# The first thirty microseconds of an attention layer: identity matmuls before the tokens come, transposes by halves of the inputs, and another order of the first loads and weight sums

## The chip, the core and the metric

The kernel runs on one core of a Trainium2 chip. The core has five engines that run side by side, each with its own queue of instructions: TensorE (PE in the profile) multiplies matrices, VectorE (DVE) and ScalarE (ACT) work element by element, GpSimd (POOL) here mostly issues DMAs, and SyncE (SP) issues DMAs only. The metric is the device time of one execution in microseconds. The kernel before took a median of 1350.63 us in three runs (1345.75, 1350.63, 1352.09).

## The reference

A layer norm, an attention with rotary positions and a fixed rescaling of some keys, a small mixture of low-rank experts whose output is a gate, and a residual sum. Cut to what matters:

```
x = L0_attn_hidden_states                      # 8 sequences x 256 tokens x 512, float32
xn = (x - mean(x)) / sqrt(var(x) + 1e-5)
q, k, v = xn @ wq.T, xn @ wk.T, xn @ wv.T      # 32 query heads, 8 key/value heads, width 128
q, k = rope(q), rope(k)
scores = q @ k.T / sqrt(128) * key_scale + causal
s = (softmax(scores) @ v) @ wo.T
logits = xn @ router_w.T                       # 4 experts, the best 2 are kept
gates = softmax(top2(logits))
delta = sum_e gates_e * (xn @ A_e.T) @ B_e.T * 4
x = x + s * silu(delta)
```

## The kernel before

**Tiling.** The 8 sequences are taken in four pairs (`tb` 0 to 3). A pair's 512 tokens are four tiles of 128 tokens (`t` 0 to 3; tiles 0 and 1 are sequence `b` = 0, tiles 2 and 3 are `b` = 1). The normalised tokens are turned, so that the 512 inputs stand on partitions, into `XB[tb]`, four blocks of 128x512: sequence `b` by half `h` of the inputs. Everything is float32, and a float32 matmul shows as two records of PE in the trace, a transpose as one.

**Products.** Weights come in quads of four blocks (A11, A12, A21, A22; numbers 0, 1, 3 and 2 in the names). A quad is multiplied with the pair of sequences in the Strassen-Winograd manner, with seven products instead of eight (`quad`, pieces p1, p2, p6, p5, p7, p4, p3). That needs four sums of weight blocks (`blocks_of`: S1 = A21+A22 is block 4, S2 = S1-A11 block 5, S3 = A11-A21 goes into block 3, S4 = A12-S2 block 6) and four sums of token blocks (`add_up`: `XT` 0 to 3, the first is `XB` of sequence 1, half 0, less that of sequence 0, half 0). Both are made on VectorE. The weight sums are also written to memory by GpSimd for the later pairs ("sums<-w"). The first quad of all is that of the first four key heads, number 8: its product into bank pa is `pak` in the trace, into pd `pdk`, into pe `pek`. The first query quad follows (`paq`, `peq`, `pdq`; weights `w_0`), then the first value quad (`pav`, weights `w_10`).

**Order.** No engine's order is written by hand. The kernel hands jobs to a planner (`Plan`): each with an engine, a planned time (`takes`), the jobs that it comes after, the buffers that it opens and closes, and a lag until its result is there. TensorE's jobs get due times from the order in which they are laid (`lay`); the others' due times follow backwards from those. `Plan.run` then plays the program through with these numbers and emits, on each engine, the ready job that is due first. So a changed number or dependency can change the order of any queue. On the chip the engines run these fixed orders and wait for each other through semaphores.

**The start, for the first pair.** `norm(0)` loads the four tiles of x on SP's queue (`load`, line 325). VectorE takes each tile's statistics (st, mv), then for two tiles at a time a variance, ScalarE's square root and a reciprocal (rstd), and it normalises (`normalise`, xn, line 348). TensorE turns a tile with the identity in four transposes (`turn`, line 355, xp), and ScalarE copies the result out of PSUM (`read`, line 366). GpSimd writes the identity at about 1 us and later clears `probs_sb` (`clear`, line 1354; "MEMSET p" in the trace). SP issues, in this order: four x, then w_8 blocks 0, 1, 3, 2, then ra (router and expert weights), then w_0 blocks 0, 1, 3, 2. ScalarE's queue issues the loads of tab and bt (rope tables and expert weights) right after its first two copies.

VectorE's order at the start: statistics of tiles 0 and 1, xn 0, xn 1, statistics of tiles 2 and 3, the weight sum of block 4, the variance of tiles 2 and 3, the sum of block 5, the reciprocal, the sums of blocks 3 and 6, xn 2, xn 3, the first key output (`ck<-pek,p1k`), XT 0 to 3.

TensorE's order: transposes of tiles 0 and 1 (8), `pak` (block 0 with sequence 0, half 0), `pek` (block 1 with sequence 0, half 1), transposes of tiles 2 and 3 (8), the router's products for two tiles (`lme`, 16 records), `pdk` (block 4 with XT 0), `pak` (block 5 with XT 1), and so on.

All instructions but a few are recorded under line 118, a helper that keeps them in program order; they are told apart by their tiles.

Of the kernel before, what the change touches and what calls it, by code (L numbers as in the profile page):

```python
# [37 lines left out]
F32 = mybir.dt.float32  # L38
# [6 lines left out]
P = 128  # L45
B, S, D = 8, 256, 512
# [10 lines left out]
NT = TB // P  # L57
DC = D // P
# [111 lines left out]
class Plan:  # L170
# [10 lines left out]
    def add(self, engine, takes, what, after=(), opens=(), closes=(), near=None, lag=0.0):  # L181
        after = [a for a in after if a]
        job = Job(engine, takes, what, after, opens, closes, near, lag, len(self.jobs))
        for a in after:
            a.then.append(job)
        for hold in closes:
            hold.readers += 1
        self.jobs.append(job)
        return job

    def lay(self, job):
        job.due = self.laid
        self.laid += job.takes
# [63 lines left out]
def layer(ctx: ExitStack, tc: tile.TileContext, x, wquad, woquad, raT, bT, table, out):  # L257
    nc = InOrder(tc)
    pool = lambda name, bufs, **kw: ctx.enter_context(tc.tile_pool(name=name, bufs=bufs, **kw))
# [9 lines left out]
    ps_mm = pool("ps_mm", 4, space=PSUM)  # L269
    ps_sc = pool("ps_sc", 2, space=PSUM)  # L270
    ps_av = pool("ps_av", 2, space=PSUM)
    bounce = pool("bounce", 4, space=DRAM)
    turned = pool("turned", 2, space=DRAM)
# [3 lines left out]
    ra = keep.tile([P, DC, E + E * R], F32, tag="ra", name="ra")  # L277
    bt = keep.tile([E * R, O], F32, tag="bt", name="bt")
    ident = keep.tile([P, P], F32, tag="ident", name="ident")
# [11 lines left out]
    plan = Plan()  # L291
    add = plan.add
    rooms = {}

    def hold(tag):
        return Hold(rooms[tag])

    for tag, n in dict(
        mm=4, sc=2, av=2, x=XPAIRS, m=2, acc=ACC, side=3, w=RING, wo=RING_O, a=RING_A, c=2, sw=2, qT=3,
# [6 lines left out]
    gates, sums_of, acts, weights, x_hold, loaded = {}, {}, {}, {}, {}, {}  # L306
# [7 lines left out]
    def norm(tb):  # L314
# [4 lines left out]
        xs, box = {}, {}  # L319
        xh = [hold("x") for _ in range(NB)]  # L320
        mh = [hold("m") for _ in range(NT)]
        ph = [hold("mm") for _ in range(0 if tb else NT)]
        x_hold[tb] = hold("X")

        def load(t):
            if t % 2 == 0:
                xs["x", t // 2] = x_pool.tile([P, 2, D], F32, tag="x", name=f"x{tb}_{t}")
            xs[t] = xs["x", t // 2][:, t % 2, :]
            nc.sync.dma_start(out=xs[t], in_=x[bass.ds(tb * TB + t * P, P), :])
# [22 lines left out]
                op0=ALU.subtract, op1=ALU.mult,  # L352
            )

        def turn(t):
            pt = box["p", t] = ps_mm.tile([P, 2, 2, P], F32, tag="mm", name=f"xp{tb}_{t}")
            for c in range(DC):
                nc.tensor.transpose(pt[:, c // 2, c % 2, :], box[t][:, bass.ts(c, P)], ident)

        def new_acts():  # L360
            acts[tb] = (
# [1 line left out]
                one.tile([P, 4, 2, S], F32, tag="XT", name=f"XT{tb}"),  # L363
            )

        def read(t):
            if t == 0:
                new_acts()
            nc.scalar.copy(acts[tb][0][:, t // 2, :, :, bass.ts(t % 2, P)], box["p", t])

        def turn_blocks(t):

# [35 lines left out]
        issues = []  # L408
        for t in range(NT):
            issues.append(  # L410
                add("sp", 0.3, lambda t=t: load(t), after=issues[-1:],
                    opens=[xh[t // 2]] if t % 2 == 0 else [])
            )
        loads = [
            add("dma", 0.0, lambda: None, after=[issues[t]], lag=8.5 if tb else 3.9 + 0.5 * t)
            for t in range(NT)
        ]
        if not tb:
# [2 lines left out]
        xn = []  # L421
        for ts in [slice(0, NT)] if tb else [slice(0, 2), slice(2, NT)]:
# [8 lines left out]
            for t in tiles:  # L431
                xn.append(
                    add("dve", 0.45, lambda t=t: normalise(t), after=[inv], opens=[mh[t]],
                        closes=[xh[t // 2]])
                )
        reads, pieces = [], []
        if tb:
            for b in range(NB):
                turns = [
                    add("dve", 0.6, lambda t=t: turn_blocks(t), after=xn[2 * b : 2 * b + 2], closes=[mh[t], xh[b]])  # L440
                    for t in (2 * b, 2 * b + 1)
# [3 lines left out]
                    add("sp", 2.4, lambda b=b: gather(b), after=[out_] + reads[:1],  # L445
                        opens=[] if b else [x_hold[tb]], lag=7.0)
                ] * 2
        for t in [] if tb else range(NT):
            tp = add("pe", 0.5, lambda t=t: turn(t), after=[xn[t], identity], opens=[ph[t]], closes=[mh[t]])
            opens = [x_hold[tb]] if t == 0 else []  # L450
            after = [tp] + reads[:1]
            reads.append(
                add("act", 0.5, lambda t=t: read(t), after=after, opens=opens, closes=[ph[t]],
                    near=(tp, 0.5))
            )
            pieces.append(tp)
        t1 = add("dve", 0.61, lambda: add_up(0), after=reads)
# [4 lines left out]
        if not tb:  # L462

            loaded["ra"] = add(
                "sp", 0.3, lambda: nc.sync.dma_start(out=ra, in_=raT), after=issues, lag=6.0
            )
            loaded["turned"] = pieces[-1]
            loaded["tab"] = add("act", 1.0, load_tables, after=reads[:1], lag=6.0)
        return pieces

# [2 lines left out]
    def blocks_of(tb, room, ring, source, kept, key, form, first):  # L473


        n = f"{room}{tb}_{key}"
        box, there, holds = {}, {}, {}
        order = (A11, A12, A21, A22, S1, S2, S4) if first else form.order
        if not tb and not first:
            order = (A11, A21, A22, A12, S1, S2, S4)  # L480

        def load(i):
            w = box[i] = ring.tile([P, 2, 2 * P], F32, tag=room, name=f"{n}_{i}")
            k = form.sums.index(i) if tb and i in form.sums else None
            src = source[:, i] if k is None else kept[:, k].rearrange("p (c m) -> p c m", c=2)
            (nc.sync if first else nc.gpsimd).dma_start(out=w, in_=src)

        def sum_up(i):
            to, a, b, op = form.steps[i]
            if to not in box:  # L490
                box[to] = ring.tile([P, 2, 2 * P], F32, tag=room, name=f"{n}_{to}")
            getattr(nc.vector, op)(box[to], box[a], box[b])

        def keep_sum(i):
            k = form.sums.index(i)
            nc.gpsimd.dma_start(
                out=kept[:, k].rearrange("p (c m) -> p c m", c=2), in_=box[i]
            )

        for i in order:  # L500
            holds[i] = hold(room)
        if tb:
            for i in order:
                after = [sums_of[room, key, i]] if i in form.sums else []
                there[i] = add("pool", 0.8, lambda i=i: load(i), after=after, opens=[holds[i]], lag=6.0)
            return box, holds, there
        issue = list(first)
        for i in order[:4]:
            there[i] = add(
                "sp" if first else "pool", 0.4 if first else 0.8, lambda i=i: load(i), after=issue,  # L510
                opens=[holds[i]], lag=6.0,
            )
        for i, (to, a, b, op) in enumerate(form.steps):
            there[to] = add(
                "dve", 0.61, lambda i=i: sum_up(i), after=[there[a], there[b]] + form.before(i, there),
                opens=[holds[to]] if to in order[4:] else [], closes=[holds[a], holds[b]],
            )
        for i in form.sums:
            sums_of[room, key, i] = add(
                "pool", 0.8, lambda i=i: keep_sum(i), after=[there[i]], closes=[holds[i]],  # L520
                lag=5.0,
            )
        return box, holds, there

    class Features:


        order = (A11, A12, S2, S1, S3, A22, S4)
# [10 lines left out]
    class Outputs:  # L539


        order = (A11, A21, S2, S1, A12, S4, A22)
# [10 lines left out]
    def quad(tb, which, out, room, rows, name):  # L553

        wbox, wh, there = blocks_of(
            tb, "w", w_pool, wquad[which], sums[which], which, Features,
            [] if len(weights) > 1 else begun,
        )  # L560
        weights[tb, which] = True
        box = {}
        new = lambda what: ps_mm.tile([P, 2, S], F32, tag="mm", name=f"{what}{name}")
        XB, XT = acts[tb, "B"], acts[tb, "T"]
        pa, pd, pe = hold("mm"), hold("mm"), hold("mm")
# [19 lines left out]
        def piece(bank, i, half, b, t, first, after):  # L585
            return add(
                "pe", 1.73, lambda: product(bank, i, half, b, t, first),
                after=[there[i]] + (XB[2 * b : 2 * b + 2] if t is None else [XT[t]]) + after,
                opens=[{"pa": pa, "pd": pd, "pe": pe}[bank]] if first else [],
                closes=[wh[i], x_hold[tb]],  # L590
            )
# [14 lines left out]
        if not tb:  # L606
# [6 lines left out]
            closes=[pe, s1], near=(p2, 1.0),  # L613
# [8 lines left out]
            closes=[s3], near=(p7, 1.0),  # L622
# [4 lines left out]
            closes=[pa], near=(p4, 0.0),  # L627
# [4 lines left out]
            near=(p3, 1.0),  # L632
# [565 lines left out]
    def experts(tb):  # L1198
# [3 lines left out]
        box = {}  # L1202
# [62 lines left out]
        routes = []  # L1265
        for t in range(NT):
            routes.append(
                add("pe", 0.94, lambda t=t: route(t),
                    after=[acts[tb, "B"][t], loaded["ra"], loaded["turned"]] + routes[:1],
                    opens=[] if t else [lh], closes=[x_hold[tb]])  # L1270
            )
        p1 = routes[-1]
# [3 lines left out]
            after=[r1], near=(p1, 4.0),  # L1276
# [77 lines left out]
    def clear():  # L1354
        nc.gpsimd.memset(probs_sb, 0.0)

    identity = add("pool", 1.5, lambda: make_identity(tc.nc, ident), near=None)
    cleared = add("pool", 2.0, clear)

    LAG_V = 2  # L1360
# [4 lines left out]


    tiles = norm(0)
    lead = []
    for q in quads[0]:
# [5 lines left out]
    for n in range(len(steps) + 2):  # L1375
        last = n >= len(steps)
        tb, g = (NTB, 0) if last else steps[n]
# [67 lines left out]
```

## Time and profile before

| | |
|---|---|
| median of three runs | 1350.63 us (1345.75 to 1352.09) |
| profiled execution | 1350.19 us, its span 1348.4 us, mean granted clock 0.998 |
| TensorE busy | 1325.3 us, 98% of the span |
| weight loads busy | 1165.7 us, 86% |
| VectorE, ScalarE, GpSimd busy | 82%, 45%, 23% |
| first transpose, first matmul, first record of pdk | 6.64, 9.35, 19.19 us from the span's start |
| landing of the last w_8 block | 11.19 us |

The span is the time from the first to the last instruction of the profiled execution; its own time holds 1.8 us more around the span. "Idle before" in a row of the profile is the time for which the engine had nothing to run before that row, with what released it behind an arrow. A row for DMA issues gives the time from the issue to the landing of the data.

### The profile page before, as it was taken

The numbers are of one execution on the slowest core, as the hardware profiler recorded it, in microseconds if no ns is written. First come the engines' busy times: TensorE is split into PE (matmuls) and PEld (weight loads), VectorE is DVE, ScalarE is ACT, GpSimd is POOL, SyncE is SP. The second block draws the span as 40 slices with busy tenths as digits, with TensorE's granted clock in tenths as the row PEclk, the third lists the DMA queues.
The fourth block names the chain that finished last, engine by engine and source line by source line (L and its number), as shares of the span: only waits on it lengthen the run. The fifth ranks groups of instructions, "written<-read, shape, count | busy, mean of one in ns | idle before, by whom it ended". The sixth has DMA issues, their size and how long they took to land.

```text
span 1348.4 us, 19893 instructions
## 1 busy us (share of the span) xinstructions
PE 1325.3 (98%) x6464; PEld 1165.7 (86%) x6464; DVE 1104.6 (82%) x2835; ACT 611.1 (45%) x1576; POOL 314.3 (23%) x579
## 2 busy tenths in 40 slices
PE   7999999999999999999999999999999999999998
PEld 6887888888889888888888988888888898888886
DVE  6899989998888768789697886969869787686997
ACT  3465444543534535354353443535444454434531
POOL 2322222222222122222222122222122211222010
PEclk9999999999999999999999999999999999999999
DMA  6577767686856666768676676676866676666584
GB/s 199 169 244 249 218 186 239 207 265 206 254 166 200 220 209 183 229 214 215 197 230 196 207 215 202 185 231 203 246 203 202 218 219 202 195 188 199 140 284 133
DMA packets 134182, 282.10 MB, mean 209 GB/s; under 512 B 40832, under 2 KB 80896, under 8 KB 134080
## 3 DMA queue, kind: packets, MB, share of 16 engines
q0 software_dynamic: 45760, 149.98, 35.9%
q1 hardware_dynamic: 88096, 130.19, 31.8%
q8 instruction: 52, 0.85, 0.2%
q10 hardware_dynamic: 224, 0.66, 0.2%
q14 instruction: 50, 0.41, 0.1%
HBM read 197.94 MB, written 82.84 MB: 208 GB/s over the span
## 4 chain that ended last, share of the span: by engine, by line
PE 75%; DVE 14%; DMA 6%; SPq 2%; issue 1%; ACT 1%; DVEq 0%; ACTq 0%
PE po L118 20%; PE paq L118 14%; PE av L118 9%; PE sc L118 7%; PE pdq L118 6%; DMA pT<-there 4%; PE pak L118 4%; PE pav L118 4%; PE peq L118 3%; DVE blocks L118 2%; PE pdk L118 2%; DVE acc L118 2%; SPq L118 2%; DVE qTq L118 2%; DVE p L118 2%; PE pdv L118 2%
## 5 line engine op out<-in xcount | busy, mean ns | idle before, releaser
L118 ACT ACTIVATE p<-z,least 128x256 f32<-128x256 f32 (+7 forms) x512 | 207.6, 407 | 203.0 <-DVE least L118 130.2
L118 PE MATMUL po<-wo,a 128*128 128x256 f32 x992 | 233.0, 379 | 0.0
L118 PEld LDWEIGHTS po<-wo,a 128*128 128x128 f32 x992 | 186.6, 190 | 22.9
L118 PE MATMUL av<-pT,v 128*128 128x256 f32 x768 | 186.3, 382 | 8.0 <-DMA pT<-there 8.0
L118 PE MATMUL paq<-XT,w 128*128 128x256 f32 x768 | 182.1, 380 | 0.3 <-ACT u3q L118 0.3
L118 DVE CUSTOM_DVE_ANT_0 z<-sc,tab 128x256 f32<-128x256 f32 (+7 forms) x512 | 134.4, 301 | 55.9 <-PE sc L118 52.8
L118 PE MATMUL po<-wo,s 128*128 128x256 f32 x744 | 177.6, 382 | 0.2 <-PE av L118 0.2
L118 PEld LDWEIGHTS av<-pT,v 128*128 128x128 f32 x768 | 145.6, 191 | 29.6 <-issue 5.6
L118 PEld LDWEIGHTS sc<-kk,qTq 128*128 128x128 f32 x1024 | 159.1, 191 | 12.8 <-DVE p L118 0.8
L118 PE MATMUL sc<-kk,qTq 128*128 128x256 f32 (+7 forms) x1024 | 168.1, 302 | 0.1
L118 PEld LDWEIGHTS paq<-XT,w 128*128 128x128 f32 x768 | 144.7, 190 | 20.2 <-ACT u2q L118 0.8
L118 POOL DMA_DIRECT2D w<-sums x144 | 79.2, 550 | 349.7 <-PE paq L118 143.9
L118 PEld LDWEIGHTS po<-wo,s 128*128 128x128 f32 x744 | 139.3, 190 | 23.4 <-issue 5.5
L118 ACT COPY a<-av 128x512 f32<-128x512 f32 x128 | 74.1, 580 | 180.5 <-PE av L118 180.2
L118 DVE TENSOR_TENSOR acc<-acc,po 128x512 f32<-128x512 f32 x189 | 127.9, 677 | 33.0 <-PE po L118 31.6
L118 ACT COPY swq<-cq 64x1024 f32<-64x1024 f32 x128 | 133.7, 1045 | 15.3 <-DVE cq L118 11.1
L118 POOL DMA_DIRECT2D w<-in_wquad_dram x148 | 80.9, 548 | 244.3 <-PE paq L118 85.2
L118 DVE STREAM_TRANSPOSE blocks<-p 128x1024 f32<-128x1024 f32 (+1 forms) x128 | 124.0, 970 | 0.2
L118 DVE TENSOR_SCALAR p<-p,total 128x256 f32<-128x256 f32 (+7 forms) x512 | 117.3, 295 | 2.3
L118 DVE TENSOR_TENSOR qTq<-cq,tab 128x1024 f32<-128x1024 f32 x64 | 78.0, 1219 | 25.3 <-ACT cq L118 25.1
L118 ACT ACTIVATION_READ_ACCUMULATOR p<-z,least 128x1 f32 x512 | 95.8, 187 | 0.0
L118 POOL DMA_DIRECT2D wo<-in_woquad_dram x104 | 56.9, 548 | 130.8 <-PE po L118 120.7
(135 smaller groups left out, 1855.0 us busy)
## 6 DMA issues: line engine op xcount, KB each, us to landing
there<-blocks SPq DMA_DIRECT2D x256, 192.0 KB, 3.9
pT<-there SPq DMA_DIRECT2D x64, 768.0 KB, 6.1
w<-in_wquad_dram POOLq DMA_DIRECT2D x148, 256.0 KB, 4.6
w<-sums POOLq DMA_DIRECT2D x144, 256.0 KB, 4.0
wo<-in_woquad_dram POOLq DMA_DIRECT2D x104, 256.0 KB, 5.0
wo<-osums POOLq DMA_DIRECT2D x96, 256.0 KB, 4.7
sums<-w POOLq DMA_DIRECT2D x48, 256.0 KB, 4.1
osums<-wo POOLq DMA_DIRECT2D x32, 256.0 KB, 5.0
```

What stands on the lines that cost most here:

```text
L118: ins = what(*args, **kwargs)
```

## The change

It has five parts.

1. TensorE's first job, `warm`, multiplies the identity with itself twelve times (24 records) into a PSUM tile that nobody reads. It waits for the identity alone, and it is laid ahead of everything.
2. Each transpose job handles a sequence and a half of the inputs instead of a tile (`turn(b, half)`): two tiles, two transposes each, into a tile of 128x512. The copy out (`read`) then fills one block of `XB`, and a product waits for its own block only, `XB[2 * b + half]`, instead of both blocks of its sequence. The job waits for both normalised tiles of its sequence.
3. SP's order becomes x 0, x 1, w_8 block 0, w_8 block 1, x 2, x 3, w_8 block 3, ra, w_8 block 2, and w_0 as before.
4. The sums of the first weights wait for the normalised tokens (`loaded["xn"]`): VectorE's order becomes ... statistics of tiles 2 and 3, variance, reciprocal, xn 3, xn 2, then the sums of blocks 4, 5, 3, 6, then ck and XT 0 to 3. In the first two tiles, too, xn 1 now comes ahead of xn 0.
5. The planner's costs and lags of these jobs are other numbers.

In the built programs the queues differ only so: PE in the twelve matmuls and the transposes; SP and VectorE as told; on ScalarE the loads of tab and bt stand after the second square root and the first copy `p1k`; and at about 35 us on VectorE the sum of block 4 of the first value quad (`w_10`) stands ahead of kk and cq of the second sequence instead of behind them. All else has the same order in both, to the end. GpSimd's order is the same throughout.

```diff
+    def then(self, before, job):
+        before.then.append(job)
+        job.waits += 1
...
-        def turn(t):
-            pt = box["p", t] = ps_mm.tile([P, 2, 2, P], F32, tag="mm", name=f"xp{tb}_{t}")
-            for c in range(DC):
-                nc.tensor.transpose(pt[:, c // 2, c % 2, :], box[t][:, bass.ts(c, P)], ident)
+        def turn(b, half):
+            pt = box["p", b, half] = ps_mm.tile([P, 2, S], F32, tag="mm", name=f"xp{b}_{half}")
+            for t in range(2):
+                for c in range(2):
+                    nc.tensor.transpose(
+                        pt[:, c, bass.ts(t, P)], box[2 * b + t][:, bass.ts(2 * half + c, P)], ident
+                    )
...
-            nc.scalar.copy(acts[tb][0][:, t // 2, :, :, bass.ts(t % 2, P)], box["p", t])
+            nc.scalar.copy(acts[tb][0][:, b, half], box["p", b, half])
...
         loads = [
-            add("dma", 0.0, lambda: None, after=[issues[t]], lag=8.5 if tb else 3.9 + 0.5 * t)
+            add("dma", 0.0, lambda: None, after=[issues[t]],
+                lag=8.5 if tb else (2.3, 2.6, 3.6, 4.0)[t])
             for t in range(NT)
         ]
...
-        for t in [] if tb else range(NT):
-            tp = add("pe", 0.5, lambda t=t: turn(t), after=[xn[t], identity], opens=[ph[t]], closes=[mh[t]])
+        for b, half in [] if tb else ((0, 0), (0, 1), (1, 0), (1, 1)):
+            tp = add(
+                "pe", 0.9, lambda b=b, h=half: turn(b, h), after=xn[2 * b : 2 * b + 2] + [identity],
+                opens=[ph[2 * b + half]], closes=mh[2 * b : 2 * b + 2],
+            )
...
+            loaded["turned"], loaded["xn"] = pieces[-1], xn[-1:]
...
-        for i in order[:4]:
+
+        lead = first and not weights
+        issue = list(first[1:2] if lead else first)
+        for k, i in enumerate(order[:4]):
...
+            issue = [add("sp", 0.45, lambda i=i: load(i), after=issue, opens=[holds[i]])]
             there[i] = add(
-                "sp" if first else "pool", 0.4 if first else 0.8, lambda i=i: load(i), after=issue,
-                opens=[holds[i]], lag=6.0,
-            )
+                "dma", 0.0, lambda: None, after=issue,
+                lag=4.5 if lead and k < 2 else 5.5,
+            )
+            if lead and k == 1:
+                plan.then(issue[0], first[2])
+                issue = first[3:]
...
-                "dve", 0.61, lambda i=i: sum_up(i), after=[there[a], there[b]] + form.before(i, there),
+                "dve", 0.61, lambda i=i: sum_up(i),
+                after=[there[a], there[b]] + form.before(i, there) + (loaded["xn"] if first else []),
...
-                after=[there[i]] + (XB[2 * b : 2 * b + 2] if t is None else [XT[t]]) + after,
+                after=[there[i]] + ([XB[2 * b + half]] if t is None else [XT[t]]) + after,
...
+    def warm():
+
+        ps = ps_sc.tile([P, P], F32, tag="sc", name="warm")
+        for _ in range(12):
+            nc.tensor.matmul(ps, lhsT=ident, rhs=ident, start=True, stop=True)
+
     identity = add("pool", 1.5, lambda: make_identity(tc.nc, ident), near=None)
+    warmed = hold("sc")
+    lay_first = add("pe", 4.0, warm, after=[identity], opens=[warmed], closes=[warmed])
+    plan.lay(lay_first)
```

More of the change, by code (lines that the diff above doesn't have):

```diff
@@ L364, in new_acts, with read @@
             )
-        def read(t):
-            if t == 0:
+        def read(b, half):
+            if b == half == 0:
                 new_acts()
-            nc.scalar.copy(acts[tb][0][:, t // 2, :, :, bass.ts(t % 2, P)], box["p", t])
+            nc.scalar.copy(acts[tb][0][:, b, half], box["p", b, half])
         def turn_blocks(t):
@@ L410, in norm @@
             issues.append(
-                add("sp", 0.3, lambda t=t: load(t), after=issues[-1:],
+                add("sp", 0.45, lambda t=t: load(t), after=issues[-1:],
                     opens=[xh[t // 2]] if t % 2 == 0 else [])
@@ L447, in norm @@
                 ] * 2
-        for t in [] if tb else range(NT):
-            tp = add("pe", 0.5, lambda t=t: turn(t), after=[xn[t], identity], opens=[ph[t]], closes=[mh[t]])
-            opens = [x_hold[tb]] if t == 0 else []
-            after = [tp] + reads[:1]
+        for b, half in [] if tb else ((0, 0), (0, 1), (1, 0), (1, 1)):
[3 more added lines that the diff above has]
+            )
             reads.append(
-                add("act", 0.5, lambda t=t: read(t), after=after, opens=opens, closes=[ph[t]],
-                    near=(tp, 0.5))
+                add("act", 0.5, lambda b=b, h=half: read(b, h), after=[tp] + reads[:1],
+                    opens=[] if reads else [x_hold[tb]], closes=[ph[2 * b + half]], near=(tp, 0.5))
             )
@@ L464, in norm @@
             loaded["ra"] = add(
-                "sp", 0.3, lambda: nc.sync.dma_start(out=ra, in_=raT), after=issues, lag=6.0
+                "sp", 0.45, lambda: nc.sync.dma_start(out=ra, in_=raT), after=issues, lag=7.0
             )
-            loaded["turned"] = pieces[-1]
+            loaded["turned"], loaded["xn"] = pieces[-1], xn[-1:]
             loaded["tab"] = add("act", 1.0, load_tables, after=reads[:1], lag=6.0)
@@ L507, in blocks_of @@
         issue = list(first)
-        for i in order[:4]:
+        lead = first and not weights
+        issue = list(first[1:2] if lead else first)
+        for k, i in enumerate(order[:4]):
+            if not first:
+                there[i] = add(
+                    "pool", 0.8, lambda i=i: load(i), after=issue, opens=[holds[i]], lag=6.0
+                )
+                continue
+            issue = [add("sp", 0.45, lambda i=i: load(i), after=issue, opens=[holds[i]])]
             there[i] = add(
-                "sp" if first else "pool", 0.4 if first else 0.8, lambda i=i: load(i), after=issue,
-                opens=[holds[i]], lag=6.0,
-            )
+                "dma", 0.0, lambda: None, after=issue,
+                lag=4.5 if lead and k < 2 else 5.5,
+            )
+            if lead and k == 1:
+                plan.then(issue[0], first[2])
+                issue = first[3:]
         for i, (to, a, b, op) in enumerate(form.steps):
             there[to] = add(
-                "dve", 0.61, lambda i=i: sum_up(i), after=[there[a], there[b]] + form.before(i, there),
+                "dve", 0.61, lambda i=i: sum_up(i),
+                after=[there[a], there[b]] + form.before(i, there) + (loaded["xn"] if first else []),
                 opens=[holds[to]] if to in order[4:] else [], closes=[holds[a], holds[b]],
@@ L1268, in experts @@
                 add("pe", 0.94, lambda t=t: route(t),
-                    after=[acts[tb, "B"][t], loaded["ra"], loaded["turned"]] + routes[:1],
+                    after=acts[tb, "B"][t // 2 * 2 : t // 2 * 2 + 2]
+                    + [loaded["ra"], loaded["turned"]] + routes[:1],
                     opens=[] if t else [lh], closes=[x_hold[tb]])
```

## The prediction

> **What bounds the kernel now.** I read the busy rows first, then PE's waits, then the chain of waits and the order of time over the first 20 us, then the landings of the first loads and the clock.
>
> ```profile
> PE   7999999999999999999999999999999999999998
> ```
> ```profile
> PE av L118 <- DMA pT<-there: 8.0, 6, 3.0
> PE xp L118 <- DVE xn L118: 7.6, 2, 6.6
> PE pak L118 <- DMA w<-in_wquad_dram: 0.8, 1, 0.8
> ```
>
> TensorE is full in all slices but the first and the last. Its waits (total, times, longest) are two kinds: 8.0 us scattered over the run for turned probabilities, and 8.4 us in the first 17 us. Outside these it is busy from pdk at 19.19 us to the end. So what the change is worth is how much earlier the unbroken work begins, that is, when the first record of pdk starts. The chain of waits says what sets that:
>
> ```profile
> 4.02 7.17 DMA w<-in_wquad_dram
> ...
> 13.98 2.94 DVE xn L118 x2
> ...
> 16.96 0.66 PE xp L118 x4
> 17.62 1.74 PE lme L118 x16
> 19.36 1.78 PE pdk L118 x8
> ```
> ```profile
> 8.38 0.18 DVE L118 BATCH_NORM_AGGREGATE mv<-st 128x2 f32<-128x6 f32 x1
> 11.29 0.69 DVE L118 TENSOR_TENSOR w<-w,w 128x512 f32<-128x512 f32 x1 [2.73 <-DMA w<-in_wquad_dram]
> ...
> 12.70 1.27 DVE L118 TENSOR_TENSOR w<-w,w 128x512 f32<-128x512 f32 x2
> 13.89 3.02 DVE L118 TENSOR_SCALAR xn<-x,mv,rstd 128x512 f32<-128x512 f32 x2
> ```
> ```profile
> 14.80 1.82 POOL L118 MEMSET p<- 128x2048 f32 x1
> ```
>
> VectorE has the second pair's statistics at 8.56 us, then stands 2.73 us in front of a weight sum whose block lands at 11.19 us, makes four sums, and only then normalises tiles 2 and 3. The last of those took 2.55 us instead of 0.54 and ended just after GpSimd's memset. Everything behind it on TensorE waits.
>
> The clock is the second bound:
>
> ```profile
> 9.35 3.75 PE L118 MATMUL pak<-XB,w 128*128 128x256 f32 x8 [0.78 <-DMA w<-in_wquad_dram]
> 12.90 2.69 PE L118 MATMUL pek<-XB,w 128*128 128x256 f32 x8
> ...
> 19.19 1.94 PE L118 MATMUL pdk<-XT,w 128*128 128x256 f32 x8
> ```
>
> Eight records of one form start 0.427 us apart in pak and 0.216 apart in pdk: half speed and full speed. The step comes inside pek at about 14.5 us. (No clock is recorded before that, so the profile's column shows 1.00 there; the spacing decides.)
>
> **The change, part by part.** Times are from the span's start.
>
> *The first transposes* wait for both tiles now. xn 0 and 1 end at 6.95 together, where the first alone ended at 6.49 and released TensorE 0.15 later. So they start at 7.10 instead of 6.64. Four transposes take 3 x 0.213 + 0.417 = 1.06 us at half speed (spacing and length in tile 0's records), 3 x 0.109 + 0.273 = 0.60 at full speed (tile 2's). ScalarE's copy starts 0.04 later and takes 0.585; pak followed a copy by 0.16. pak starts at 7.70+0.04+0.585+0.16 = **8.48** at full speed, or 8.94 at half, against 9.35. Its weights:
>
> ```profile
> x<-in_x_dram SPq DMA_DIRECT2D x1, 256.0 KB, 4.4
> w<-in_wquad_dram SPq DMA_DIRECT2D x1, 256.0 KB, 6.6
> ```
>
> These are the fourth and fifth loads, issued at 2.12 and 2.60, landing at 6.53 and 9.22. The nine first loads landed at 3.54, 4.19, 5.58, 6.53, 9.22, 9.85, 10.53, 11.19 and 11.57. All blocks have 256 KB, so I give each load the landing of its new place: w_8 blocks 0 and 1 at 5.6 and 6.5 (no wait left), x 2 and 3 at 9.22 and 9.85, block 2 last at 11.57. The bytes that the records show moved would allow x 3 at about 8.0; that is the good end.
>
> *The identity matmuls.* 24 records from about 1.4 us. lme's records, bound by their weight loads, are 0.112 apart at full speed, so I take 0.223 at half: 5.3 us, over at 6.8, before the transposes. They delay nothing. Do they bring the clock? [...] The row: full speed came 5.15 us after pak began. [...]
>
> ```profile
> 642.55:645.97 3.42, 1.13 (x6) 0.68 (x5) 3.42 (x7) 1.13 (x2) 0.00 (x0) 1.00 0.75 262
> 645.97:649.38 3.41, 3.41 (x10) 2.70 (x9) 3.14 (x3) 0.58 (x1) 0.00 (x0) 0.50 0.26 47
> ```
>
> (Window, its length, busy time of PE, weight loads, VectorE, ScalarE, GpSimd, granted clock, DMA.) PE was busy for a third of the first window, and the next ran at 0.50. Between the last identity matmul (5.8 to 6.8) and pak (8.48) TensorE has only 0.9 us of transposes, so this can recur. Three values for the end of pek's sixteen records from 8.48: full speed, 16 x 0.216 = 3.45, 11.9; half speed through pak alone, 13.6; no clock gained (from 8.94, with the step at 14.3, as late as now), 15.0. [...]
>
> *The second pair.* x 3 at 9.85: its statistics 0.69 behind tile 2's, starting at 9.95; from there 0.69 + 0.86 (aggregate to the first xn, as for tiles 0 and 1) gives xn 3 at 11.50, xn 2 at 11.96 to 12.50. Transposes at 12.65 if PE is free, 8 x 0.109 = 0.87, then lme 1.74: TensorE could start pdk at **15.3**. With pek ending at 13.6 it is 16.2; at 15.0 it is 17.65.
>
> *The weight sums* now stand on VectorE between xn 2 and XT 0, as do ck and the sums' waits. Sums start 0.61 apart: 12.42, 13.03, 13.64, 14.25, then ck 14.86, XT 0 at 15.47 to 16.16, pdk 0.2 later: **16.4**. That is what is late next, not TensorE. If x 3 landed at 8.0, block 2 at 11.57 would set it: 15.5.
>
> *The memset* follows the fourth sum by 1.5 us (13.29 to 14.80 now), so 15.8 to 17.6, beside XT 1 to 3. Does it stop them as it stopped xn? [...] The row: xn, one tensor input, was held until the memset's end; no two-input operation lay under the memset. [...]
>
> *The rest.* tab is issued behind p1k, at about 11 to 14 instead of 8.62, and takes 5.6 us; it is first read at 27.39 now, so it is covered by 5 us or more. ra lands by 11.6, before lme. w_0 loads keep their place. The copies of the second pair wait up to 1 us behind tab's and bt's issue on ScalarE; XT 0 at 15.47 covers that. The moved sum of w_10 waits for pak-like work that ends 0.24 us before its turn (paq on w_0 block 3, 38.65 against 38.89), and its load has 3 us in hand; the cq behind it slips 0.6 us with 1.6 before pdq needs it. All three: nothing.
>
> **Sum.** pdk starts at 16.4 (bounds 15.5 and 18.5) instead of 19.19: 2.75 us less, all of it kept since TensorE is full behind. 1350.19 - 2.75 = **1347.4**. The profiled execution lies between the three runs' median (1350.63) and mean (1349.5), so I let it stand for them. What a measurement can tell from no change is about 0.5%, 6.8 us; the forecast is less than that, so "same" by this bound.
>
> **Rivals.**
> - *The clock does not come* (0.15): pdk at 17.65, 1.5 us gained, 1348.7. [...]
> - *The gain is swallowed by later waits* (0.12): the waits of av for pT are 0.8 to 3.0 us each in four places; one more like the longest gives 1350.4. For: the three runs before differ by 6.3 us with one program. Against: nothing in the change touches those transfers.
> - *They shrink* (0.07): without the 2.29 us wait at 645 us and the half-speed stretch behind it (3.41 us, half of it lost), 4.0 us more, 1343.4; without the 2.97 at 114 us too, 1340.4.
> - *Slower* (0.04): xn 2 and four sums now all stand in front of XT 0 on one queue. pdk is x 3's landing + 6.55 us, or block 2's + 3.95. From x 3 later than 12.6, or block 2 later than 15.2, the start is later than now. At 15.0 for x 3 pdk starts at 21.55, 1352.6. Against: the slowest of the first nine loads took 7.2 us, which from 3.07 is 10.3.
> - *The forecast* 0.62.
>
> **Numbers.** The forecast's own bounds are 1346.5 and 1349.5. A median of few runs moves by 2 us or so with the scatter above, so eight in ten lie within 1343.3 and 1350.8. Faster by over 0.5% needs the shrinking waits, or the forecast with part of them: 0.10. Slower by over 0.5% takes the last rival twice over, or several long waits: 0.03. Same: 0.87.
>
> **What would show it.** The identity matmuls from 1.4 to about 6.8 us or less. pak at 8.5 to 8.9, released by ScalarE, not by a DMA. pak and pek together in 3.5 to 5.2 us if the clock came, 6 if not. xn rows of 0.54 us, the memset behind the sums, XT rows of 0.69 beneath it. pdk at 16.4, behind a short wait of TensorE for VectorE. The same waits for pT later on. I am wrong if XT is held by the memset, if x 2 and 3 land after 12 us, if the clock stays half past 14 us, or if the time moves by more than the start does.

## The result and the profile after

The changed kernel took a median of 1342.39 us in ten runs (1340.55 to 1347.16); the kernel before, in ten runs beside it, 1349.03 (1344.88 to 1352.83). The ratio is 0.9963, with a 95% interval of 0.995 to 0.9976: 5.0 us faster, between 3.2 and 6.7 (the two medians lie 6.6 us apart; gains here are taken from the ratios). The profiled execution took 1345.25 us with a span of 1343.5; before, 1350.19 and 1348.4.

The busy row of the page has lost its first hole, and TensorE's waits (total, times, longest) have changed at the start alone:

```profile
PE   9999999999999999999999999999999999999998
```
```profile
PE av L118 <- DMA pT<-there: 8.2, 7, 1.8
PE warm L118 <- POOL ident masks.py:199: 1.4, 1, 1.4
PE pdk L118 <- DVE XT L118: 1.0, 1, 1.0
PE xp L118 <- DVE xn L118: 0.6, 2, 0.5
```

The 7.6 us of waiting for xn have become 0.6. In their place stands a wait of 1.0 us in front of pdk, for VectorE. TensorE in order of time (start, length, what, idle before):

```profile
1.36 5.08 PE L118 MATMUL warm<-ident 128*128 128x128 f32 x24 [1.36 <-POOL ident masks.py:199]
6.90 1.09 PE L118 MATMUL xp<-ident,xn 128*128 128x128 f32 x8 [0.46 <-DVE xn L118]
8.23 1.99 PE L118 MATMUL pak<-XB,w 128*128 128x256 f32 x8 [0.24 <-ACT XB L118]
10.06 1.89 PE L118 MATMUL pek<-XB,w 128*128 128x256 f32 x8
12.12 1.09 PE L118 MATMUL xp<-ident,xn 128*128 128x128 f32 x8 [0.17 <-DVE xn L118]
13.05 1.90 PE L118 MATMUL lme<-ra,XB 128*128 128x68 f32 x16
15.94 1.96 PE L118 MATMUL pdk<-XT,w 128*128 128x256 f32 x8 [0.99 <-DVE XT L118]
```

pak and pek run at full speed: eight records in 1.99 and 1.89 us where they took 3.75 and 2.69. pdk starts at 15.94 instead of 19.19. lme ends at 14.95, and then TensorE stands for XT. VectorE and GpSimd over the same time:

```profile
11.06 1.00 DVE L118 TENSOR_SCALAR xn<-x,mv,rstd 128x512 f32<-128x512 f32 x2
11.98 2.61 DVE L118 TENSOR_TENSOR w<-w,w 128x512 f32<-128x512 f32 x4
14.51 0.68 DVE L118 TENSOR_TENSOR ck<-pek,p1k 128x512 f32<-128x512 f32 x1
15.11 1.28 DVE L118 TENSOR_TENSOR XT<-XB 128x512 f32<-128x512 f32 x2
```
```profile
15.42 1.82 POOL L118 MEMSET p<- 128x2048 f32 x1
```

Both xn take 1.00 us together instead of 3.02, four sums and ck follow without a gap, and XT has its usual length under the memset (1.28 us for two rows, 1.29 in the kernel before without one).

So 3.25 of the 4.9 us between the two spans come from the start. The other 1.7 us are one stretch at half speed, from 645.97 to 649.38 us, that the profiled execution before had and this one has not. The experiments take the two apart.

### The profile page after: what moved, and what is told of

Same layout as the page of the kernel before. It is cut to its first block, busy times and chain, and to the rows that moved or that the text cites. A ratio compares the mean times of both kernels' runs of the same rounds, so it can differ in the third digit from the quotient of the medians.

```text
span 1343.5 us, 19943 instructions
## 1 busy us (share of the span) xinstructions
PE 1325.6 (99%) x6488; PEld 1167.2 (87%) x6488; DVE 1102.8 (82%) x2835; ACT 611.2 (45%) x1576; POOL 314.3 (23%) x579
## 4 chain that ended last, share of the span: by engine, by line
PE 80%; DVE 10%; DMA 6%; SPq 2%; issue 1%; ACT 1%; DVEq 0%; ACTq 0%
PE po L118 21%; PE paq L118 15%; PE av L118 10%; PE sc L118 8%; PE pdq L118 7%; DMA pT<-there 5%; PE peq L118 4%; PE pak L118 4%; PE pav L118 4%; PE pdk L118 2%; SPq L118 2%; PE pdv L118 2%; DVE blocks L118 2%; DVE qTq L118 1%; DVE p L118 1%; DVE acc L118 1%
## 5 line engine op out<-in xcount | busy, mean ns | idle before, releaser
L118 ACT COPY swq<-cq 64x1024 f32<-64x1024 f32 x128 | 133.7, 1044 | 14.8 <-DVE cq L118 10.7
```

Source lines behind the costliest of these rows:

```text
L118: ins = what(*args, **kwargs)
```

## The experiments

All times are set against the kernel before on the same chip, with ratio and 95% interval. pdk is the start of its first record in the profile.

**The norm ahead, alone.** One group of the planner's jobs is emitted ahead of the sum of block 4, so that no other queue changes but the second root on ScalarE, which goes ahead of two DMA issues:

```diff
+        if not tb:
+            plan.group = [v, r, inv, *xn[2:]]
```

> The kernel before, with one thing moved: variance, root, reciprocal, xn 2 and xn 3 stand on VectorE ahead of the four weight sums. Theory (two paths meet at pdk; the clock keeps TensorE's path late): xn rows of 0.54 us, over by 10.7; pak still starts at 9.35 at half speed, pek ends at about 15.4, transposes to 16.3, lme to 18.0, so pdk at 18.1 instead of 19.19, 1.1 us gained. Rival (the order of VectorE is the whole of it): pdk at 16.0, all 3.25 us. Time: 1.1 us below before by the theory, 3.3 by the rival.

pdk at 18.45, ratio 1.0007 (0.9996 to 1.0018): no gain in time, 0.5 us at most.

```profile
9.32 3.78 PE L118 MATMUL pak<-XB,w 128*128 128x256 f32 x8 [0.68 <-ACT XB L118]
12.89 3.11 PE L118 MATMUL pek<-XB,w 128*128 128x256 f32 x8
15.84 1.04 PE L118 MATMUL xp<-ident,xn 128*128 128x128 f32 x8
16.71 1.90 PE L118 MATMUL lme<-ra,XB 128*128 128x68 f32 x16
18.45 1.73 PE L118 MATMUL pdk<-XT,w 128*128 128x256 f32 x7
```

xn was over at 10.7, five microseconds before TensorE could use it. pak and pek at half speed now set the start. The clock stepped up at 15.4 in this execution, 0.9 us later than in the first profile (pek took 3.11 us instead of 2.69), hence 18.45 and not 18.1. The rival, VectorE's order as the whole of it, falls. The theory's 1.1 us is not reached either: three profiles of the kernel before (below) have pdk at 18.65 on average, 0.2 us behind this one.

**The memset first.** One due time is set, and GpSimd clears p right behind the identity:

```diff
-    cleared = add("pool", 2.0, clear)
+    cleared = add("pool", 2.0, clear, near=None)
+    cleared.due = -1.0
```

> The kernel before, with GpSimd's memset of p issued right behind the identity instead of behind the weight sums' stores. Theory (xn 3 was held by the memset, and this alone set the 19.19): xn 3 takes 0.54 us and ends at 14.9, pek ends at 15.4 as before, pdk at 18.1, the same as with the norm moved ahead. Rival (xn 3 was late for another reason, the four sums ahead of it): xn 3 still takes 2.5 us, pdk stays at 19.2. A memset at 1.3 us might instead hold an early VectorE row of statistics or xn; by the theory the two-microsecond memset is over before the first x lands at 3.5.

VectorE's order is that of the kernel before, and yet xn 2 and 3 take their plain time:

```profile
12.50 1.27 DVE L118 TENSOR_TENSOR w<-w,w 128x512 f32<-128x512 f32 x2
13.69 1.00 DVE L118 TENSOR_SCALAR xn<-x,mv,rstd 128x512 f32<-128x512 f32 x2
```
```profile
1.25 1.80 POOL L118 MEMSET p<- 128x2048 f32 x1
```

The hold was the memset's: 1.00 us for the two without it, 3.02 with it. pdk came at 17.38 and not 18.1: TensorE's path set it again, and the clock stepped up at 13.2 this time (pek took 2.09 us). In time nothing is to be seen, 1.0001 (0.9993 to 1.001), 0.9 us at most; a single profile with an early clock is not the average start.

**The identity matmuls alone.** `warm` is called in the identity's job, in the kernel before:

```diff
+    def identity_first():
+        make_identity(tc.nc, ident)
+        warm()
```

> The kernel before, with the twelve identity matmuls added and nothing else. Theory (VectorE's path sets pdk there, so TensorE's speed in pak and pek is worth nothing): pak and pek at full speed and over by about 13, then TensorE waits for xn 3 until 16.9; pdk at 19.2, no gain, time as before within 0.3 us. Rival (the clock is most of the gain): pdk at 17 to 17.5 and 1.7 to 2 us gained. If the idle stretch from 6.5 to 9.35, longer here than in the changed kernel, lowers the clock again, pak and pek stay at half speed and nothing can be said of the rival.

Ratio 1.0008 (0.9998 to 1.0019): no gain, and in the profile pdk is later than ever, at 20.11.

```profile
10.22 1.89 PE L118 MATMUL pek<-XB,w 128*128 128x256 f32 x8
13.42 0.66 PE L118 MATMUL xp<-ident,xn 128*128 128x128 f32 x4 [1.31 <-DVE xn L118]
15.89 1.11 PE L118 MATMUL xp<-ident,xn 128*128 128x128 f32 x4 [1.82 <-DVE xn L118]
16.80 3.52 PE L118 MATMUL lme<-ra,XB 128*128 128x68 f32 x16
20.11 3.72 PE L118 MATMUL pdk<-XT,w 128*128 128x256 f32 x8
```

TensorE is done with pek 3.5 us sooner than before and then waits for the same late xn. While it waits it loses its clock; the windows (length, busy time of PE, weight loads, VectorE, ScalarE, GpSimd, granted clock, DMA) show it:

```profile
11.20:14.61 3.41, 1.56 (x9) 0.87 (x7) 3.41 (x6) 1.00 (x3) 3.17 (x5) 1.00 0.96 338
14.61:18.03 3.42, 2.14 (x11) 2.14 (x11) 2.19 (x3) 0.67 (x2) 0.94 (x1) 0.50 0.85 295
18.03:21.44 3.41, 3.41 (x14) 3.19 (x14) 2.21 (x4) 0.00 (x0) 0.00 (x0) 0.50 0.03 6
21.44:24.85 3.41, 3.41 (x9) 2.70 (x8) 0.69 (x1) 0.00 (x0) 0.00 (x0) 0.50 0.00 0
24.85:28.20 3.35, 3.35 (x20) 3.03 (x19) 1.29 (x2) 0.59 (x1) 1.51 (x3) 1.00 0.21 78
```

The speed won in pak and pek was given back in lme and pdk, 3.52 and 3.72 us where the kernel before took 1.90 and 1.94. The mean granted clock of its 14 runs, 0.9962 where the kernel before has 0.9980, fits with this being no single case. It does not show it: the norm ahead alone had 0.9968 in 22 runs, with no such stretch at the start of its profile.

**Both of these.** The kernel before with the norm ahead and the identity matmuls, the two edits above:

> The kernel before with two parts of the change alone: the norm of tiles 2 and 3 ahead of the weight sums, and the twelve identity matmuls. Alone, the first moved pdk from 19.19 to 18.45 and the second to 20.11. Theory (two paths meet at pdk, and each part clears one of them): pak and pek at full speed from 8.4 to 9.3, over by 12 to 12.9, xn over by 10.7, so pdk at 14.6 to 15.3, a gain of about 4 us where the parts alone gave 0.7 and -0.9; total 4 to 6 us below before. Rival (the parts add up): pdk at 19.4, no gain; or, the halves and the order of the loads are needed: pdk at 16.5 or later.

```profile
8.86 1.96 PE L118 MATMUL pak<-XB,w 128*128 128x256 f32 x8 [1.03 <-DMA w<-in_wquad_dram]
10.66 1.89 PE L118 MATMUL pek<-XB,w 128*128 128x256 f32 x8
...
15.00 1.94 PE L118 MATMUL pdk<-XT,w 128*128 128x256 f32 x8
```

Ratio 0.9971 (0.9959 to 0.9983), 3.9 us faster. Two parts that are worth nothing alone give the start of the changed kernel together: pdk is where two paths meet, and each part clears one.

**Without the identity matmuls.** The converse, in the changed kernel:

```diff
-    lay_first = add("pe", 4.0, warm, after=[identity], opens=[warmed], closes=[warmed])
-    plan.lay(lay_first)
```

> The changed kernel without the twelve identity matmuls, all else in the same order. Theory (with the norm ahead, TensorE's path is the late one unless it has its clock): transposes at half speed, pak at 8.8, pek's end between 13.5 and 15.0 by where the clock steps up, pdk at 16.2 to 17.7, on average 1.2 us later than in the changed kernel (15.94), then without a wait for XT. Rival (VectorE's path sets pdk, the clock is hidden): pdk at 15.9 to 16.0. Time: 0.3 to 1.8 us above the changed kernel by the theory, equal by the rival.

pdk at 16.75 without a wait, pak's eight records in 3.78 us. Ratio 0.999 (0.9976 to 1.0003), 1.3 us faster than before with 3.2 at most: most of the gain in time is gone.

**The other two parts.** The loads in the old order (`lead = False`; ra moves ahead of block 1 with it):

> The changed kernel with x 2 and 3 loaded ahead of the first weights again (x 0 to 3, block 0, ra, blocks 1, 3, 2), all other queues as in the changed kernel. Theory (the order of these loads is worth little, since VectorE's path is set by the last block's landing and four sums): pak starts at 8.5 to 9.3, released by the load of block 0 instead of by ScalarE; xn 2 over by 10.3; the first sum at the landing of block 2, about 11 to 11.6; pdk at 15.0 to 15.6, no later than the changed kernel's 15.94. Rival (weights between the tokens are what keeps TensorE on time): TensorE stands still from 6.4 to 9.3 but for the transposes, its clock falls to half again, and pdk comes at 17 or later.

and the transposes by tiles (`turn(t)` and `read(t)` as before, so that pak waits for both copies):

> The changed kernel with transposes by tiles instead of by halves of the inputs, so that pak waits for both copies. Theory (this part is hidden behind VectorE's path): pak at 8.8 instead of 8.23, pek's end and the second transposes later by 0.3 to 0.5, pdk still at 15.9 to 16.0 behind a shorter wait for XT; time as the changed kernel's. Rival (the halves carry part of the gain): pdk later by the 0.5 us that pak is.

The old order of loads is no worse: pdk at 14.63 (15.3 to 15.9 in three profiles of the changed kernel), no wait in front of it, ratio 0.9956 (0.9942 to 0.997). x 3 landed at 6.68 instead of 9.25, and block 0 at 8.23 was still in time for pak at 8.37, so the stall that the rival foresaw did not come in this execution. With both parts alone, block 0 landed at 8.73 and pak waited 1.03 us for it; pdk came at 15.00. Transposes by tiles cost pak 0.6 us (8.85), which VectorE's path hides: pdk at 15.32, ratio 0.9966 (0.9951 to 0.9981).

**VectorE's next wait taken away.** XT 0 and 1 ahead of the sum of block 6 and of ck, in the changed kernel (the jobs named here are emitted ahead of that sum):

```diff
+            plan.early = [*pieces[2:], *reads[2:], t1, t2]
```

> The changed kernel with XT 0 and XT 1 on VectorE ahead of the sum of block 6 and of ck. Theory (VectorE's queue, not TensorE, sets pdk by 1.0 us): TensorE's wait in front of pdk goes, pdk at 14.8 to 15.0, right behind lme; no new wait in front of the next pak. Time 1.0 us below the changed kernel. Rival (ScalarE's second copy, or block 4's sum, would come next): pdk at 15.3 or later.

```profile
12.85 1.90 PE L118 MATMUL lme<-ra,XB 128*128 128x68 f32 x16
14.58 1.94 PE L118 MATMUL pdk<-XT,w 128*128 128x256 f32 x8
```

pdk is right behind lme and the wait is gone, as the theory had it. The time is 0.9965 (0.9954 to 0.9977). A microsecond more cannot be told from the changed kernel, which on that chip had 0.9955 (0.9941 to 0.997).

**The two kernels again, and where the rest of the time lies.** The changed kernel was timed and profiled once more beside those runs, and both kernels were profiled further:

> The changed kernel once more, beside the others of this call. First theory (all of the gain is the earlier start): pdk at 15.9 to 16.4, and the time 3.2 us below before, 1345.1 where before has 1348.3, with the clock at half speed behind waits for pT as often as in the kernel before. Second theory (the rest of the run has changed too, fewer half-speed stretches): 5 to 6 us below, 1342.5 to 1343.3, and a mean granted clock near 0.999 where before has 0.998.

> The kernel before once more, for its profile. Theory (the span is the start of paq, plus the waits for pT, plus half of the half-speed stretches, plus 1308.6 us that is the same in all kernels of this study): the sum holds within 0.4 us again. The start moves with the landing of the last weight block: pdk 5.8 to 8 us behind that landing, 17.5 to 19.5, since xn 3 is held by the memset again (about 2.5 us). Against it: a remainder that differs by over 0.5 us, or an xn 3 of 0.54 us.

> As before_2, a third profile of the kernel before: the same sum, and the scatter of its start, of its waits for pT and of its half-speed stretches. By the theory that the second gain is fewer half-speed stretches, at least one stretch of 3.4 us behind a wait of over 2 us in one of these two profiles.

> A third profile of the changed kernel: pdk at 15.2 to 16.0, behind a wait for XT of up to 1 us; the span is the start of paq, the waits for pT, half of the half-speed stretches, and 1308.6 us within 0.4.

With 0.9955 (0.9941 to 0.997) of the second set the gain was 6.1 us, again more than the start. Each profile's span can be split into the start of paq, TensorE's idle time behind it, half the length of its half-speed stretches, and a remainder:

| profile | span | paq | idle behind | half-speed loss | remainder | last w_8 block / x 3 landed | pdk |
|---|---|---|---|---|---|---|---|
| before | 1348.4 | 29.8 | 8.6 | 1.7 | 1308.3 | block 11.19 | 19.19 |
| before_2 | 1348.1 | 29.1 | 9.3 | 1.7 | 1308.0 | block 10.54 | 18.54 |
| before_3 | 1344.3 | 28.8 | 7.4 | 0 | 1308.1 | block 10.21 | 18.22 |
| after | 1343.5 | 26.5 | 8.5 | 0 | 1308.5 | x 3 9.25 | 15.94 |
| after_again | 1344.3 | 25.9 | 8.6 | 1.7 | 1308.1 | x 3 8.59 | 15.29 |
| after_3 | 1344.3 | 26.0 | 9.7 | 0 | 1308.7 | x 3 8.70 | 15.38 |
| both parts alone | 1344.9 | 25.6 | 8.8 | 1.7 | 1308.8 | | 15.00 |
| XT first | 1344.0 | 25.4 | 10.3 | 0 | 1308.3 | | 14.58 |

The remainder is the same in all fourteen profiles, 1307.9 to 1308.8. With the waits for pT alone, as the expectation had it, the remainder of after_3 is 1309.6, a miss by 1 us; all of TensorE's idle time has to be counted. The start follows a single landing in each kernel: before, pdk comes 8.0 us behind the last block in all three profiles; after, 6.7 us behind x 3 in all three. On average the start is 3.1 us earlier (18.65 against 15.54), 3.25 being the first pair's.

What is over 3.1 us is not in the start. Part of a long wait's price is in the clock. In the first profile of the kernel before, TensorE waited twice for 2.0 us or longer for pT: behind the wait of 2.29 us (up to 645.53) it ran at half speed for 3.41 us, behind that of 2.97 (up to 114.53) it did not. In the first profile of the changed kernel the longest such wait is 1.8 us, and half speed followed none. One more wait with half speed behind it, in the second profile of the changed kernel:

```profile
107.40:109.90 2.50, 0.22 (x3) 0.03 (x1) 2.43 (x12) 1.07 (x4) 0.00 (x0) 0.99 0.69 224
109.90:113.30 3.40, 3.21 (x8) 2.59 (x9) 2.86 (x3) 0.28 (x1) 0.54 (x1) 0.50 0.80 209
```

The mean granted clock of all runs is 0.9986 and 0.9987 for the changed kernel (10 and 13 runs) and 0.9980, 0.9975 and 0.9980 for the one before (51, 47 and 13). Some 0.0009 of 1346 us is 1.2 us less lost to half speed. This is a rough figure: in the five kernels with the early start that were timed beside the kernel before, the difference is 0.7 to 1.6 us, and the mean takes in the end of the span, where TensorE has nothing left to do and half speed costs nothing (1.4 and 1.5 us of clock lost there in the first profiles of the two kernels, with TensorE busy for 0.00). Why such stretches should be rarer is open: idle time behind paq is no smaller in the changed kernel's profiles (8.5 to 9.7 against 7.4 to 9.3), and no run here steered the waits. 3.1 and 1.2 make 4.3 of the 5.0 and 6.1; the rest lies within the intervals. With both parts alone the gain of 3.9 us (2.3 to 5.5) is that of its start, 18.65 - 15.00 = 3.65.

## Why the prediction was right, and where it was not

By its own steps:

- **First transposes and pak**: 7.10 and 8.48 forecast, 6.90 and 8.23 measured, released by ScalarE and no longer by a load. x had landed 0.1 us sooner, which is half of the difference.
- **Identity matmuls**: over by 6.8 forecast, 6.44 measured, because the clock came at 5.87 while they still ran (records 0.21 us apart, then 0.11). pak's eight records took 1.96 to 1.99 us in all eight profiles with identity matmuls and 3.67 to 3.78 in the six without, so the rival in which the clock does not come (0.15) was met in none; that so much work brings the clock was the author's estimate, which no run had shown beforehand. Of the three values for pek's end, 11.9, 13.6 and 15.0, the first held: 11.95. The second, half speed again through the gap of transposes in front of pak, came in no profile. The fall of the clock that the prediction feared did come in one place, behind pek in the kernel with the identity matmuls alone, where TensorE waited 1.3 and 1.8 us for xn (pdk's eight records took 3.72 us); in the seven profiles that have the norm ahead as well it did not (1.94 to 1.97).
- **Loads**: x 3 at 9.85 forecast by its place in the queue, 9.25 measured (8.59 and 8.70 in the other profiles); block 2 at 11.57 against 10.96. The rule of thumb, landing by place, was late by 0.6 to 1.3 us there, and early for blocks 0 and 1: 5.6 and 6.5 forecast, 6.62 and 7.92 measured, still ahead of pak and pek. That all nine loads have 256 KB was wrong (ra has 136), without consequence.
- **What is late next**: VectorE's sums in front of XT, forecast as x 3's landing plus 6.55 us; it was 6.7. pdk at 16.4 forecast, 15.94 measured, with a wait for XT of 1.0 where 16.4 - 15.3 = 1.1 had been worked out. 2.75 us of start became 3.25; the difference is x 3's landing.
- **Memset**: nothing forecast, nothing measured. XT rows lay under it and took 1.28 us for the first two and 1.41 for the others, against 1.29 and 1.41 clear of it in the kernel before, while xn rows of two profiles more of the kernel before were held again (3.02 us for two). The upper bound of 18.5 is an XT 0 held to the memset's end, 17.6 + 0.69 + 0.2; no run shows such a hold, and pdk came at 15.3 to 15.9 in three profiles of the changed kernel.
- **tab, bt, ra, w_0, the moved sum of w_10**: behind pdk TensorE has no wait up to 79 us but one of 0.08 there.

The weak step is in the sum: "all of it kept since TensorE is full behind", with everything behind pdk taken as equal. The start was kept whole, but the term for half-speed stretches, 1.7 us of the profiled execution's 1350.19, was carried over unchanged, and by the mean clocks some 1.2 us of such loss went. It had a place only in a rival, "they shrink", at 0.07; of that rival the clock is seen in part, the shorter waits are not. So 2.75 us stand against 5.0 (3.2 to 6.7), and what is left beyond start and clock is not explained. The forecast of 1347.4 was too high for a second reason: its base of three runs lay 1.6 us above the median of ten. The median of 1342.39 is 0.9 below the range's low end; the ratio applied to the base of the forecast, 0.9963 x 1350.63 = 1345.6, is inside. The interval leaves out 1, so there is a gain; by the forecast's bound of 0.5% it is no change, as forecast. That the forecast's 2.75 us came close to the start's 3.1 is earned by its steps; that the missing term stayed under the bound is luck.

What the forecast did not see is in the parts. It priced them in one pass through the changed kernel and never asked what each is worth alone: the order of the loads and the transposes by halves were worth nothing measurable, and the other two only together.

## What to carry to other kernels

Where two paths meet in front of the bounding engine, price every part of a change against both: a part that clears one path is worth nothing until the other is cleared, and it can look like a failure alone. Match each start to the one landing that it follows (here a constant 6.7 or 8.0 us) before believing a difference between two profiles. A wait of TensorE of 2 us or more costs its own length and can cost clock besides: 1.7 us behind the wait of 2.29 us here, nothing behind that of 2.97.

## What the runs showed of the hardware

- Half speed came and went here in steps of 3.413 us: in the first profiles of both kernels the clock's changes lie a whole number of these apart (14.50, 645.97, 649.38 and 1345.70 us before, 185, 1 and 204 steps; 5.87 and 1340.48 after, 391). On that grid, in the middle of the run, TensorE's three emptiest windows held 1.13, 1.50 and 1.91 us of work before, and 1.89, 2.01 and 2.19 after; the clock fell behind the one with 1.13 alone. The wait of 2.29 us lay in that window whole, that of 2.97 us was split between two, 1.92 and 1.05. The prediction shows the window with 1.13 us and the half speed behind it; here is the one with 1.50, from the same profile, and the next at full speed. They share the wait of 2.97 us:

```profile
110.06:113.48 3.42, 1.50 (x10) 1.23 (x8) 3.35 (x14) 1.06 (x4) 0.00 (x0) 1.00 0.77 286
113.48:116.89 3.41, 2.36 (x11) 2.13 (x12) 3.21 (x4) 0.79 (x2) 0.54 (x1) 1.00 0.77 208
```

- At the start one window does not fit: that at 11.2 us with the identity matmuls alone, 1.56 us busy and half speed behind it, where 1.50 kept full speed above. Of these, 0.66 us are transposes and some 0.9 are pek. What sets it apart is not shown.
- The way up took more. In both first profiles TensorE was busy for all 3.41 us of the window in front of full speed, 11.09 to 14.50 before and 2.46 to 5.87 after, there with identity matmuls alone. The window before it in the kernel before, 7.67 to 11.09, with 2.64 us (0.90 of them transposes), still had half speed behind it; the one behind it in the changed kernel, 5.87 to 9.29, kept full speed with 2.72 (1.09 of them transposes).
- Half speed outlasted full work once. With the identity matmuls alone, the stretch from 18.03 to 21.44 us had TensorE busy throughout (3.41 us) and was still followed by another at half speed; most of it was lme, with 68 moving columns, and the weight loads were busy for 3.19 us of it. After a whole stretch of 256-column products (21.44 to 24.85, 3.41 us busy) the clock returned, 1.00 from 24.85. This is one case, and no run shows what part lme has in it.
- xn, an operation with one tensor input and scalars beside it, was held under GpSimd's memset in all four profiles where both met, three of the kernel before and that of the identity matmuls alone: 3.02 us for two rows instead of 1.00, over 0.29 us behind the memset's end each time. Sums of two tensors were not: two rows of XT took 1.28 us and two more 1.41 under it in the changed kernel, 1.29 and 1.41 clear of it in the kernel before.
- The nine first loads, eight of 256 KB and ra of 136, issued some 0.45 us apart, land some 0.65 us apart at the end of the row (ra some 0.37 behind the load ahead of it), but somewhere between the second and the fifth there is a jump, 2.69 us in front of the fifth in the first profile of the kernel before and some 2.5 in front of the third in that of the changed kernel, and it differs between executions: the last w_8 block landed at 11.19, 10.54 and 10.21 in three profiles of the kernel before, and pdk moved with it, 19.19, 18.54 and 18.22.
